# Edge attention on a graph: ScalarE's round in another order, one exp in place of two, and a third PSUM bank for small results

## The chip, the core and the metric

One core of a Trainium2 chip runs the whole program. The metric is the device time of one execution in microseconds. A profiled execution adds a trace: every instruction of the engines TensorE (PE, its weight loads PEld), VectorE (DVE), ScalarE (ACT), GpSimd (POOL) and SyncE (SP), and every DMA.

## The reference

6250 nodes with 128 features, 206250 edges sorted by their destination, 8 heads of 16 columns.

```python
Qh, Kh, Vh = (h @ WQ), (h @ WK), (h @ WV)        # each [N, 8, 16]
Eh = edge_attr @ WE                              # [E, 8, 16]
score = einsum('ehd,ehd,ehd->eh', Kh[src], Qh[dst], Eh) / sqrt(16)
score = exp(clip(score, -5, 5))
wV = segment_sum(Vh[src] * score[:, :, None], dst)
Z = segment_sum(score, dst)
x = layernorm(x + wV / (Z + 1e-6))
```

## The kernel before, in words

The edges lie in tiles of 128, one edge per partition, and four tiles are a batch: 406 batches, the last few of them smaller. First TensorE makes a table kv (K and V of each node, 256 columns) and stores it to HBM. Then one loop runs over the batches, and in each step every engine works at a different batch. In the steady part the code's order is each engine's order (`manual_schedule`).

- **Rows of the source nodes** (`gather`): GpSimd issues one indirect DMA per tile, which reads 128 rows of kv into the tile kvrows. 1426 of them are issued: a few tiles per batch are made in other ways. One is a *column tile*: VectorE and ScalarE copy x's columns one by one into xcol (`run`, `columns`), TensorE multiplies xcol by the weights into the PSUM tile colkv (`project_columns`), and ScalarE places the result in kvrows (`place_columns`). In a few batches SyncE loads the rows of one tile one by one. The first gather of a batch b from 18 on is held back until TensorE has done Q's rows of batch b - lag(b):

```python
return max(STEP, 12 - (b - LOCK) // 32)          # lag(b): STEP 3, LOCK 18
```

- **Q's rows** (`stage_0t`, `mark_t`, `stage_a`): TensorE makes marks_t, ScalarE turns it into onehotT by a Relu, and TensorE multiplies onehotT by a window of Q's table into qps. marks_t has one PSUM bank, so the next batch's marks_t waits for this onehotT. `build_q` makes the table, with qrows in PSUM and four VectorE instructions.
- **Scores** (`products`, `scores`): VectorE multiplies kvrows by qps, and that by eps (the edges' features times WE), sums by head and clips: sc, 32 columns per batch. qps and eps have one bank each.
- **Weights** (`weigh`): ScalarE takes exp of sc twice, once into exp_p, a single tile in PSUM, and once into the last 8 columns per tile of msg (128 + 8 columns, in SBUF, three buffers).
- **Messages** (`messages`): VectorE multiplies V's half of kvrows by exp_p, each of the 8 weights repeated over 16 columns, into the first 128 columns of msg.
- **Sums** (`stage_0`, `mark`, `stage_c`): TensorE makes marks, ScalarE the one-hot of the destinations, one for two batches, and TensorE multiplies it by msg into agg. ScalarE copies agg out (sum), `finish` shifts the sums into place (finps) for a block of 128 nodes, and VectorE's `layernorm` is spread over the steps by `fill`.

In step b VectorE runs the products of b - 1, the scores of b - 2 and the messages of b - 3, with pieces of columns between them. ScalarE's part of the step begins with the exps of b - 2. The PSUM pool psT (tag oT) has two banks, which marks, colkv, finps and qrows take in turn. The messages of b - 3 read exp_p, and the exps of b - 2 write it again in the same step.

Of the kernel before, what the change touches and what calls it, by code (L numbers as in the profile page):

```python
# [8 lines left out]
F32 = mybir.dt.float32  # L9
# [3 lines left out]
AF = mybir.ActivationFunctionType  # L13
ALU = mybir.AluOpType
AX = mybir.AxisListType

P = 128
N, E, D, H, DH = 6250, 206250, 128, 8, 16
NT = (E + P - 1) // P
EPAD = NT * P  # L20
B = 4
# [125 lines left out]
def edge_attention(ctx: ExitStack, tc: tile.TileContext, x, xT, srcT, srcA, srcV, srcR, dstT, dstB, dst0, bnd, loB, onB, onQ, eaT,  # L147
                   wq, wkv, we, out, kv, qtab, qs, relD, relO):
    nc = tc.nc
# [27 lines left out]
    nbat = len(batches)  # L177
# [9 lines left out]
    with ExitStack() as fast:  # L187
# [104 lines left out]
        sp = fast.enter_context(tc.tile_pool(name="sums", bufs=7))  # L292
        psE = fast.enter_context(tc.tile_pool(name="psE", bufs=1, space=bass.MemoryType.PSUM))
        psQ = fast.enter_context(tc.tile_pool(name="psQ", bufs=1, space=bass.MemoryType.PSUM))
        psT = fast.enter_context(tc.tile_pool(name="psT", bufs=2, space=bass.MemoryType.PSUM))
        psA = fast.enter_context(tc.tile_pool(name="psA", bufs=2, space=bass.MemoryType.PSUM))
        psX = fast.enter_context(tc.tile_pool(name="psX", bufs=1, space=bass.MemoryType.PSUM))
        psM = fast.enter_context(tc.tile_pool(name="psM", bufs=1, space=bass.MemoryType.PSUM))
        rows5 = [cp.tile([MR, P], BF16, name=f"rows5{i}") for i in range(3)]
        for tl in rows5:  # L300
            nc.vector.memset(tl, 1.0)
        exp_p = psX.tile([P, B, H], F32, name="exp_p")

        def pair_bank(i, name, shape):

# [75 lines left out]
        def load_rel(c):  # L381

            if c < NJ and c not in rels:
                rels[c] = rows_q[c % 3]
                nc.sync.dma_start(rels[c][:3], relD[c])
# [4 lines left out]
        def load_chunk(c):  # L390
            if c in chunks or c * CH >= NT:
                return
            n = min(CH, NT - c * CH) * P
            tl = ep.tile([P, CH * P], F32, name="ea")
            nc.sync.dma_start(tl[:, :n], eaT[:, c * CH * P:c * CH * P + n])
            chunks[c] = tl
# [35 lines left out]
        def due(b, v, part):  # L432

            n = int((b + part - 1 - COL0 + COLL) * COLP[1] * share[v] / COLP[0] + 1e-6) // (1 + v) * (1 + v)
            return min(n, len(col_batches) * share[v])

        def copy(v):

            c, (k, i) = copied[v] % COLN, divmod(copied[v], share[v])
            if c == 0:  # L440
                addresses(v)
                at_hand[v] = ahead[v].pop(0)
            copied[v] += 1 + v
            if k not in col_tiles:
                col_tiles[k] = wp.tile([P, P], F32, name="xcol", bufs=6)
            to, at = col_tiles[k], at_hand[v]
            if v:
                i += share[0]
                nc.vector.tensor_tensor(to.bitcast(I32)[:, i:i + 2], column(at[c], 8, I32),  # L449
                                        column(at[c + 1], 8, I32), op=ALU.bitwise_or)  # L450
            else:
                nc.scalar.copy(to[:, i:i + 1], column(at[c], 4, F32))  # L452

        def columns(b, part=1.0):

            while copied[0] < due(b, 0, part):
                copy(0)
# [45 lines left out]
        def place_columns():  # L503

            while projected:
                g, pk = projected.pop()
                nc.scalar.copy(g[:, B - 1, :], pk)  # L507
# [39 lines left out]
        def load_rows(c):  # L547

            if c < NJ and c not in rows_in:
                rows_in.add(c)  # L550
                nc.sync.dma_start(rows5[c % 3][:3 * WT], relO[c].rearrange("r (t e) -> (r t) e", t=WT))
# [48 lines left out]
        def mark_t(b):  # L600

            if b not in marks_t:
                return
            m, n = marks_t.pop(b)
            ohTs[b] = wp.tile([QROWS, B * P], BF16, name="onehotT", bufs=4)
            nc.scalar.activation(ohTs[b][:, :n * P], m[:, :n * P], AF.Relu)  # L606
# [35 lines left out]
        def weigh(b):  # L642

            n, g, sc = st8[b]
            nc.scalar.activation(exp_p[:, :n], sc[:, :n], AF.Exp, scale=0.25)  # L645
            m = wp.tile([P, B, MW], F32, name="msg")
            nc.scalar.activation(m[:, :n, D:], sc[:, :n], AF.Exp, scale=0.25)  # L647
            st8[b] = [n, g, m]
# [27 lines left out]
        def messages(b):  # L676
            n, g, m = st8[b]
            nc.vector.tensor_tensor(  # L678
                m[:, :n, :D].rearrange("p b (h d) -> p b h d", h=H),
                g[:, :n, D:].rearrange("p b (h d) -> p b h d", h=H),  # L680
                exp_p[:, :n, :, None].to_broadcast([P, n, H, DH]), op=ALU.mult)

        def stage_c(b):
            (n, g, m), oh = st8.pop(b), ohs.pop(b)
# [70 lines left out]
        for b in range(nbat + 4):  # L755
            on = b < nbat
            if b >= XB and not manual:
                manual.append(fast.enter_context(tc.manual_schedule()))
            held += [(b + SLAG, store) for store in stores]
            stores.clear()  # L760
            if held and (held[0][0] <= b or b >= nbat):
                held.pop(0)[1]()
            if b < nbat:
                load_chunk(batches[b][0] // CH + EB - 3)
                if batches[b][0] % WT == 0:
                    load_rows(batches[b][0] // WT + 1)
                    load_rel(batches[b][0] // WT + 2)
                load_q(batches[b][0] // WT + QLOOK)
                g = gathered.pop(b)
                if b == min(XB, nbat - 1):  # L770
                    late_loads()
                if b in (12, 13):
                    next(window, None)
                if b == 14:
                    for _ in window:
                        pass
                    window = from_window(1) if NJ > P else iter(())
                    next(window, None)
                if b >= 20 and b % 4 == 0:
                    next(window, None)  # L780
                if b == 0:
                    for u in range(min(2, nbat)):
                        stage_0t(u)
                        mark_t(u)
                stage_a(b, g)
                if b + GLEAD < nbat and b + GLEAD not in gathered:
                    gathered[b + GLEAD] = gather(b + GLEAD)
            norms.extend(late)
            late[:] = pending
            pending.clear()  # L790
            if b >= nbat:
                norms.extend(late)
                late.clear()
            made = products(b - 1) if 0 <= b - 1 < nbat else iter(())
            summed = scores(b - 2) if 0 <= b - 2 < nbat else iter(())
            if on and b >= XB:
                load_single(b, 0.5)
            next(made, None)
            for _ in run(b, 0.5) if on else ():
                fill(False)  # L800
            fill(False)
            next(made, None)
            next(summed, None)
            for _ in run(b, 1.0) if on else ():
                fill()
            fill()
            fill()
            next(summed, None)
            if 0 <= b - 3 < nbat:
                messages(b - 3)  # L810
            if 0 <= b - 2 < nbat:
                weigh(b - 2)
            while qwork and b > XB and qwork[0][1] < 3:
                build_q(0, False)
            place_columns()
            if 0 <= b - 1 < nbat:
                stage_0(b - 1)
            if b + 2 < nbat:
                stage_0t(b + 2)
            if b < nbat:  # L820
                columns(b)
            mark(b - 1)
            if b + 2 < nbat:
                mark_t(b + 2)
            for _ in range(len(ready) if b >= nbat - 2 else 1):
                if ready:
                    finish(ready.pop(0))
            if b == min(60, nbat):
                count_inside()
            if 0 <= b - 3 < nbat:  # L830
                stage_c(b - 3)
            if b < nbat:
                load_single(b, 1.0)
                project_columns(b + GLEAD)
                place_rows(b + GLEAD)
                build_q(q_built(min(NJ - 1, batches[b][0] // WT + QLOOK + 2)), True)
                if not qwork and len(built) < q_built(
                        min(NJ - 1, batches[min(nbat - 1, b + 3)][0] // WT + QLOOK + 2)):
                    qwork.append([q_rows(len(built)), 1])
                    next(qwork[0][0])  # L840
            if b == min(80, nbat + 1):
                inside = nc.values_load(cnt_i[0:1, 0:1], min_val=0, max_val=2 * EPAD,
                                        skip_runtime_bounds_check_because="two counts of EPAD edges")
# [190 lines left out]
```

## Time and profile before

| | us |
|---|---|
| median of three runs | 1878.13 |
| lowest and highest | 1872.55, 1889.53 |
| the profiled execution | 1871.11 |
| its span | 1869.3 |

| engine | busy us | share of the span |
|---|---|---|
| VectorE | 1648.0 | 88% |
| TensorE | 1499.8 | 80% |
| ScalarE | 1495.3 | 80% |
| GpSimd | 1359.8 | 73% |

A row of a group reads: line, engine, operation, out<-in by the program's names, shapes, count; then the busy time of all and the mean of one in ns; then the engine's idle time just before them, and what ended most of it. "issue" is idle time for which the profile shows no releaser. A row of a timeline begins with start and duration in us. A row of stretches has the stretch, its length, the busy time, the count in brackets, TensorE's granted clock, the DMA share and GB/s. A row of waits has the waiting instruction, the releaser, the total, the count and the longest.

### The profile page before, as it was taken

To read this page: it belongs to the slowest core of one execution; us is meant where nothing else is said; L and a number is where in the kernel's file an instruction comes from. 1 tells how busy PE (TensorE), PEld (TensorE's weight loads), DVE (VectorE), ACT (ScalarE), POOL (GpSimd) and SP (SyncE) were. 2 spreads that over 40 slices of the span, in tenths; PEclk is the share of its full clock that TensorE was granted. 3 is DMA by queue.
4 is the path that set the end of the run, shared out by engine and by line. 5 is a ranking of instruction groups with operands and counts; after the bars stand their busy time and mean duration, and the time that the engine had idled before them with its cause. 6 is when DMAs were issued, how large, how long until landed. Compare 5 with 4: busy or idle time off the path is not lost.

```text
span 1869.3 us, 54198 instructions
## 1 busy us (share of the span) xinstructions
PE 1499.8 (80%) x10000; PEld 1206.9 (65%) x10000; DVE 1648.0 (88%) x8774; ACT 1495.3 (80%) x11631; POOL 1359.8 (73%) x1433
## 2 busy tenths in 40 slices
PE   6898878878787888888887878877888878777886
PEld 4676657666666666666676666756766656666765
DVE  6468998898889988999989999899899899999986
ACT  3446888788898888898888888888888988988962
POOL 7767767777777776777766777777777777777774
PEclk9888898899899998999989999899989999999897
DMA  8655556556555655655555556556555556566652
GB/s 292 214 163 161 163 173 188 165 179 183 170 178 177 183 172 162 184 180 174 181 173 163 177 174 183 176 167 177 173 174 180 179 175 185 177 178 183 198 153 67
DMA packets 169255, 329.59 MB, mean 176 GB/s; under 512 B 67440, under 2 KB 95156, under 8 KB 168904
## 3 DMA queue, kind: packets, MB, share of 16 engines
q0 software_dynamic: 67664, 183.79, 33.0%
q1 hardware_dynamic: 100115, 141.48, 24.9%
q14 instruction: 272, 2.22, 0.4%
q8 instruction: 80, 1.31, 0.3%
q10 hardware_dynamic: 1124, 0.79, 0.1%
HBM read 309.03 MB, written 16.88 MB: 174 GB/s over the span
## 4 chain that ended last, share of the span: by engine, by line
DVE 34%; ACT 17%; PE 13%; DMA 8%; issue 7%; DVEq 6%; POOL 4%; SPq 2%; ACTq 2%; POOLq 0%
ACT xcol L452 12%; DVE xcol L449 10%; DMA kvrows<-kv,src 7%; DVEq L420 6%; DVE kq L629 5%; DVE sc L636 5%; DVE msg L678 5%; DVE kq L627 5%; POOL kvrows L518 4%; PE agg L700 4%; PE eps L620 3%; ACT onehot L584 2%; PE finps L659 2%; ACT onehotT L606 2%; ACTq L420 1%
## 5 line engine op out<-in xcount | busy, mean ns | idle before, releaser
L518 POOL DMA_INDIRECT kvrows<-kv,src x1378 | 1309.8, 950 | 471.6 <-issue 308.0
L452 ACT COPY xcol<-xz 128x1 f32 x9802 | 991.4, 189 | 76.9 <-issue 66.9
L700 PEld LDWEIGHTS agg<-msg,onehot 128*128 128x128 f32 x3224 | 436.0, 203 | 318.3 <-DVE msg L678 119.1
L449 DVE TENSOR_TENSOR xcol<-xz 128x2 int32 x5915 | 508.9, 152 | 60.5 <-issue 58.3
L620 PE MATMUL eps<-we_sb,ea 128*128 128x128 f32 x3224 | 489.4, 298 | 71.8 <-DVE kq L629 69.8
L700 PE MATMUL agg<-msg,onehot 128*128 128x136 f32 x3224 | 518.5, 307 | 32.3 <-DVE msg L678 30.6
L620 PEld LDWEIGHTS eps<-we_sb,ea 128*128 128x128 f32 x3224 | 424.2, 205 | 100.4 <-DVE kq L629 94.5
L627 DVE TENSOR_TENSOR kq<-kvrows,qps 128x512 f32<-128x512 f32 x406 | 273.8, 674 | 63.5 <-PE qps L615 38.8
L597 PE MATMUL marks_t<-rows_q,steps_q 5*126 5x512 bf16 x406 | 161.8, 399 | 169.5 <-ACT onehotT L606 155.5
L629 DVE TENSOR_TENSOR kq<-kq,eps 128x512 f32<-128x512 f32 x406 | 271.1, 668 | 8.6 <-PE eps L620 6.5
L678 DVE TENSOR_TENSOR msg<-kvrows,exp_p 128x512 f32<-128x512 f32 x406 | 272.7, 672 | 6.2 <-ACT exp_p L645 6.2
L636 DVE TENSOR_REDUCE sc<-kq 128x32 f32<-128x512 f32 x406 | 271.9, 670 | 0.3
L606 ACT ACTIVATE onehotT<-marks_t 126x512 bf16<-126x512 f32 x406 | 235.9, 581 | 19.2 <-PE marks_t L597 18.9
L645 ACT ACTIVATE exp_p<-sc 128x32 f32<-128x32 f32 x406 | 80.9, 199 | 193.9 <-DVE msg L678 191.1
L615 PE MATMUL qps<-qw,onehotT 126*128 126x128 bf16 x1612 | 168.8, 229 | 10.9 <-DVE kq L627 10.9
L615 PEld LDWEIGHTS <-onehotT 126*128 126x128 bf16 x1612 | 134.5, 103 | 47.8 <-issue 21.7
L500 PE MATMUL colkv<-wkv_sb,xcol 128*128 128x256 f32 x338 | 116.2, 429 | 17.2 <-ACT onehot L584 17.2
L584 ACT ACTIVATE onehot<-marks 128x512 f32<-128x512 f32 (+2 forms) x206 | 119.0, 577 | 5.5 <-PE marks L563 5.4
L659 PEld LDWEIGHTS finps<-sum,shift 128*128 128x128 f32 x640 | 81.4, 198 | 40.3 <-ACT kvrows L507 20.9
L659 PE MATMUL finps<-sum,shift 128*128 128x136 f32 x640 | 91.4, 296 | 9.5 <-ACT kvrows L507 9.5
L647 ACT ACTIVATE msg<-sc 128x32 f32<-128x32 f32 x406 | 88.5, 218 | 0.0
L639 DVE TENSOR_SCALAR sc<-sc 128x32 f32<-128x32 f32 x406 | 80.9, 199 | 0.9
(88 smaller groups left out, 799.3 us busy)
## 6 DMA issues: line engine op xcount, KB each, us to landing
ea<-eaT SPq DMA_DIRECT2D x201, 512.0 KB
rowkv<-kv SPq DMA_DIRECT2D x2176, 1.0 KB
kvrows<-kv,src POOLq DMA_INDIRECT x1378
qw<-qs SPq DMA_DIRECT2D x202, 31.5 KB
kv<-ea SPq DMA_DIRECT2D x12, 512.0 KB
qs<-qst SPq DMA_DIRECT2D x48, 96.0 KB
rows_q<-relD SPq DMA_DIRECT2D x202, 6.0 KB
rows<-relO SPq DMA_DIRECT2D x202, 6.0 KB
```

The costliest lines, as they stand in the source:

```text
L449: nc.vector.tensor_tensor(to.bitcast(I32)[:, i:i + 2], column(at[c], 8, I32), column(at[c + 1], 8, I32), op=ALU.bitwise_or)
L452: nc.scalar.copy(to[:, i:i + 1], column(at[c], 4, F32))
L518: ins = nc.gpsimd.indirect_dma_start(out=g[:k, i, :f], out_offset=None, in_=rows, in_offset=bass.IndirectOffsetOnAxis(ap=src_col(t)[:k], a ...
L606: nc.scalar.activation(ohTs[b][:, :n * P], m[:, :n * P], AF.Relu)
L615: expanded[b] = nc.tensor.matmul(pq[:, i, :], ohT[:, i * P:i * P + P], loaded[t0 // WT], start=True, stop=True)
L620: nc.tensor.matmul(pe[:, i, :], ea[:, i * P:i * P + P], we_sb, start=True, stop=True)
L627: nc.vector.tensor_tensor(t0[:, :n], g[:, :n, :D], pq[:, :n], op=ALU.mult)
L629: nc.vector.tensor_tensor(t0[:, :n], t0[:, :n], pe[:, :n], op=ALU.mult)
L636: nc.vector.tensor_reduce(sc[:, :n], t0[:, :n].rearrange("p b (h d) -> p b h d", h=H), axis=AX.X, op=ALU.add)
L659: nc.tensor.matmul(ps, shift[:, P - s:2 * P - s], sums[k // 2][:, k % 2], start=first and i == 0, stop=stop and i == len(parts) - 1)
L678: nc.vector.tensor_tensor(m[:, :n, :D].rearrange("p b (h d) -> p b h d", h=H), g[:, :n, D:].rearrange("p b (h d) -> p b h d", h=H), exp_p[ ...
L700: nc.tensor.matmul(aggs[u][:, 0 if final else k % 2], oh[:, i, :], m[:, i, :], start=not final and t % (2 * G) == 0, stop=tail)
```

## The change

Three things: the exp into exp_p and its tile are gone, and the messages read the weights from msg's own last columns; psT has three banks, the third being the one that exp_p had; and the place of three calls in the step is another, so that ScalarE runs the one-hots first, then the exps, the placing of column tiles and the columns.

```diff
-        psT = fast.enter_context(tc.tile_pool(name="psT", bufs=2, space=bass.MemoryType.PSUM))
+        psT = fast.enter_context(tc.tile_pool(name="psT", bufs=3, space=bass.MemoryType.PSUM))
...
-        psX = fast.enter_context(tc.tile_pool(name="psX", bufs=1, space=bass.MemoryType.PSUM))
...
-        exp_p = psX.tile([P, B, H], F32, name="exp_p")
...
             n, g, sc = st8[b]
-            nc.scalar.activation(exp_p[:, :n], sc[:, :n], AF.Exp, scale=0.25)
             m = wp.tile([P, B, MW], F32, name="msg")
             nc.scalar.activation(m[:, :n, D:], sc[:, :n], AF.Exp, scale=0.25)
...
                 g[:, :n, D:].rearrange("p b (h d) -> p b h d", h=H),
-                exp_p[:, :n, :, None].to_broadcast([P, n, H, DH]), op=ALU.mult)
+                m[:, :n, D:, None].to_broadcast([P, n, H, DH]), op=ALU.mult)
...
-            if 0 <= b - 2 < nbat:
-                weigh(b - 2)
             while qwork and b > XB and qwork[0][1] < 3:
                 build_q(0, False)
-            place_columns()
             if 0 <= b - 1 < nbat:
                 stage_0(b - 1)
             if b + 2 < nbat:
                 stage_0t(b + 2)
-            if b < nbat:
-                columns(b)
             mark(b - 1)
             if b + 2 < nbat:
                 mark_t(b + 2)
+            if 0 <= b - 2 < nbat:
+                weigh(b - 2)
+            place_columns()
+            if b < nbat:
+                columns(b)
```

ScalarE, about a step and a half late in the program, before (L645 and L647 are the exps, L452 the columns, L420 loads of the columns' addresses, L507 the placing of a column tile, L584 and L606 the one-hots):

```order
L645 ACTIVATE exp_p<-sc 128x32
L647 ACTIVATE msg<-sc 128x4x8
L507 COPY kvrows<-colkv 128x256
L452 COPY xcol<-xz 128x1 x2
L420 TENSOR_LOAD col_at_82
L452 COPY xcol<-xz 128x1 x16
L420 TENSOR_LOAD col_at_82
L452 COPY xcol<-xz 128x1 x9
L584 ACTIVATE onehot_78<-marks 128x2x4x64
L606 ACTIVATE onehotT<-marks_t 126x512
```

The same step now (lines are two or three lower from here on: L582 and L604 are the one-hots, L644 the exp, L505 the placing, L450 the columns):

```order
L582 ACTIVATE onehot_78<-marks 128x2x4x64
L604 ACTIVATE onehotT<-marks_t 126x512
L644 ACTIVATE msg<-sc 128x4x8
L505 COPY kvrows<-colkv 128x256
L450 COPY xcol<-xz 128x1 x2
L418 TENSOR_LOAD col_at_82
L450 COPY xcol<-xz 128x1 x16
L418 TENSOR_LOAD col_at_82
L450 COPY xcol<-xz 128x1 x9
```

The two one-hots moved from the end of the step to its start, one exp of the two is left, and the copies behind them are the same.

VectorE, one step late in the program, before (L639 is the clip, L678 the messages, L627 and L629 the two products, L449 pieces of columns, L636 the sum by head):

```order
L639 TENSOR_SCALAR sc<-sc 128x32
L678 TENSOR_TENSOR msg<-kvrows,exp_p 128x4x128
L627 TENSOR_TENSOR kq<-kvrows,qps 128x512
L420 TENSOR_LOAD col_at_83
L449 TENSOR_TENSOR xcol<-xz 128x2 x8
L629 TENSOR_TENSOR kq<-kq,eps 128x512
L636 TENSOR_REDUCE sc<-kq 128x32
```

And now:

```order
L637 TENSOR_SCALAR sc<-sc 128x32
L675 TENSOR_TENSOR msg<-kvrows,msg 128x4x128
L625 TENSOR_TENSOR kq<-kvrows,qps 128x512
L418 TENSOR_LOAD col_at_83
L447 TENSOR_TENSOR xcol<-xz 128x2 x8
L627 TENSOR_TENSOR kq<-kq,eps 128x512
L634 TENSOR_REDUCE sc<-kq 128x32
```

Nothing moved on VectorE; the messages' second operand is msg in place of exp_p. The rows of TensorE and GpSimd are the same in the steady part of both programs.

## The prediction

> **What bounds the kernel now.** I read the page first, for who is busy and with what.
>
> ```profile
> span 1869.3 us, 54198 instructions
> ...
> PE 1499.8 (80%) x10000; PEld 1206.9 (65%) x10000; DVE 1648.0 (88%) x8774; ACT 1495.3 (80%) x11631; POOL 1359.8 (73%) x1433
> ...
> DVE 34%; ACT 17%; PE 13%; DMA 8%; issue 7%; DVEq 6%; POOL 4%; SPq 2%; ACTq 2%; POOLq 0%
> ...
> L518 POOL DMA_INDIRECT kvrows<-kv,src x1378 | 1309.8, 950 | 471.6 <-issue 308.0
> ...
> L452 ACT COPY xcol<-xz 128x1 f32 x9802 | 991.4, 189 | 76.9 <-issue 66.9
> ...
> L678 DVE TENSOR_TENSOR msg<-kvrows,exp_p 128x512 f32<-128x512 f32 x406 | 272.7, 672 | 6.2 <-ACT exp_p L645 6.2
> ...
> L645 ACT ACTIVATE exp_p<-sc 128x32 f32<-128x32 f32 x406 | 80.9, 199 | 193.9 <-DVE msg L678 191.1
> ```
>
> By busy time VectorE leads with 88%, and its share of the chain, the line that begins with DVE, is the largest. GpSimd looks idle a quarter of the time. But the row of the gathers (L518) has 471.6 us of idle time that mostly nobody released ("issue"). So I read GpSimd next: the line's own view (durations as min/median/max), and from its timeline the first gather and a stretch near the end.
>
> ```profile
> L518 POOL DMA_INDIRECT kvrows<-kv,src x1378: 900/946/1912, 67.4 to 1847.5; - x197
> ...
> 3.62 1.11 POOL L518 DMA_INDIRECT kvrows<-x,src  x1 [2.06 <-DMA src<-srcT]
> ...
> 1739.86 0.95 POOL L518 DMA_INDIRECT kvrows<-kv,src  x1 [0.30 <-PE eps L620]
> ...
> 1847.52 0.90 POOL L518 DMA_INDIRECT kvrows<-kv,src  x1 [0.30 <-PE marks_t L597]
> ```
>
> From 1739.86 to 1847.52 us stand 87 gathers, 86 intervals, so one per 1.25 us: 0.946 of work, the median, and 0.304 that passes even where nobody is waited for. GpSimd is **saturated** there, whatever its busy share says. There are 1378 gathers from kv and 48 from x, 1426 in all, and 1426 x 1.25 = 1782.5 us. With 3.6 us before the first and 20.9 us behind the last (1847.52 + 0.90 to 1869.3) this makes 1807.0 us: the floor of this program while it issues 1426 gathers. The other 62.3 us are gathers that waited or took long. Where they waited, the groups of that engine in two stretches and in an early part of the first say:
>
> ```profile
> L518 POOL DMA_INDIRECT kvrows<-kv,src x922 | 875.9, 950 | 325.5 <-issue 208.9 <-PE qps L615 28.1 <-DVE qst L348 13.0
> ...
> L518 POOL DMA_INDIRECT kvrows<-kv,src x412 | 390.7, 948 | 128.3 <-issue 88.7 <-DVE sc L639 5.4 <-DVE xcol L449 3.7
> ...
> L518 POOL DMA_INDIRECT kvrows<-kv,src x189 | 181.3, 959 | 69.3 <-issue 47.6 <-PE marks_t L597 8.1 <-DVE kq L629 3.0
> ```
>
> The first row is the time from 130 to 1330 us. Less 0.304 us for each gather, 45.2 us of waiting are left. The second, 1330 to 1848 us, has 3.0 us left. The third, 130 to 380 us, has 11.8 of the first row's 45.2. The program holds each batch's first gather until TensorE has reached Q's rows of a batch some way back; that distance falls from 12 batches to 3. So up to 1330 us the other engines set the pace and GpSimd waits for them; behind that, GpSimd sets it. How fast the others go is counted by VectorE's first product (L627), one per batch; the x is the count:
>
> ```profile
> 1000.00:1300.00 300.00, 46.10 (x68) 0.95 0.58 175
> 1500.00:1800.00 300.00, 47.09 (x70) 0.97 0.61 183
> ```
>
> 68 batches in 300 us are 4.41 us each. GpSimd needs 1426 / 406 x 1.25 = 4.39 us per batch. The race is nearly even, so both sides of the change must be priced.
>
> **The change part by part.** *What it takes from the other engines.* The waits that it can end stand in the view of waits:
>
> ```profile
> ACT exp_p L645 <- DVE msg L678: 191.1, 143, 5.0
> PE marks_t L597 <- ACT onehotT L606: 155.5, 162, 2.3
> DVE kq L627 <- PE qps L615: 38.8, 30, 9.4
> DVE qst L348 <- PE qrows L344: 38.1, 29, 2.5
> PE qrows L344 <- ACT onehot L584: 21.0, 17, 2.3
> PE colkv L500 <- ACT onehot L584: 17.2, 17, 2.2
> PE finps L659 <- ACT kvrows L507: 9.5, 15, 1.0
> ```
>
> Dropping the first of the two exps takes 406 x 199 ns = 80.9 us from ScalarE, and with the single exp_p tile goes the wait for the messages, 191.1 us. Neither is on GpSimd's path, so by themselves they are worth nothing. Moving the one-hots ahead of the exps and the columns' copies takes away what TensorE waits for: onehotT no longer stands behind some 24 copies (9802 / 406), so most of the 155.5 us go. The third bank serves the last three rows, 21.0 + 17.2 + 9.5 = 47.7 us at most. These TensorE waits also count only by what they let VectorE do sooner: its waits for TensorE are 38.8 + 38.1 us, and 9.4 of them are one start-up wait that stays. That leaves 67.5 us, over 406 batches 0.17 us each. If all go, the pace is 4.41 - 0.17 = 4.24 us; if none, 4.41. I take most of it, since late onehotT and the two-bank rows stand directly ahead of these matmuls.
>
> The move has a wait of its own: ScalarE's round now starts at the one-hots, which need marks_t, a TensorE matmul behind the batch's edge products (eps). Behind them queue the exp, the placing of a column tile and the columns' copies. The exp is wanted by the messages one step (some 4 us) later and the columns several batches later, so I cost it at nothing. If the cover failed, VectorE would wait at the messages, where it now waits 6.2 us in all. VectorE's, TensorE's and GpSimd's orders are unchanged in the steady part, and no DMA moves, so no queue is passed.
>
> *What it costs: the messages read two SBUF tiles.* Their second operand was exp_p in PSUM and is now msg's own last 8 columns in SBUF. The instruction's length I bound from rows: 672 ns now (L678, 512 elements with one PSUM operand); the two-SBUF rows below, 0.41 us for 256 elements and 1.23 for 1024, put 512 at 0.68. At most 10 ns by 406, or 4 us of VectorE, which waits anyway. The larger cost is what such an instruction does to a gather:
>
> ```profile
> 122.26 1.23 DVE L233 TENSOR_TENSOR ea<-ea,relo 128x1024 f32<-128x1024 f32 x1
> ...
> 122.48 1.82 POOL L518 DMA_INDIRECT kvrows<-kv,src  x1 [4.73 <-DVE ea L232]
> ...
> 631.19 0.41 DVE L939 TENSOR_TENSOR h<-h,xb 128x256 f32<-128x256 f32 x1
> ...
> 631.23 1.19 POOL L518 DMA_INDIRECT kvrows<-kv,src  x1 [0.30 <-DVE h L936]
> ...
> 562.56 0.41 DVE L939 TENSOR_TENSOR h<-h,xb 128x256 f32<-128x256 f32 x1
> ...
> 562.45 0.95 POOL L518 DMA_INDIRECT kvrows<-kv,src  x1 [0.30 <-DVE h L936]
> ...
> 402.64 0.41 DVE L936 TENSOR_TENSOR h<-fin,rz 128x256 f32<-128x256 f32 x1
> ...
> 402.86 1.00 POOL L518 DMA_INDIRECT kvrows<-kv,src  x1 [0.30 <-issue]
> ```
>
> L233 and L939 read two SBUF tiles. The gather at 631.23 took 1.19 in place of 0.95, 0.24 more; L939 ended at 631.60, so the gather stood still from 631.36, 0.13 us behind its start, to that end. At 122.48 the same: 0.87 longer, L233's end at 123.49, so again 0.13 behind the start. At 562.45 the product began 0.11 us after the gather, and nothing happened. So a gather needs something at 0.13 us that a two-SBUF product holds, once that product has begun by about 0.03 us ahead of the gather (the latest that stretched one, at 631.19, by 0.04). A message of 0.67 us then catches a gather whose start lies in a window of 0.67 - 0.13 - 0.03 = 0.51 us out of each 1.25, that is 41% of them, and delays it half of 0.51 on the mean: 0.41 x 0.255 = 0.105 us per message, 42.6 us for 406. Bounds: nothing, if the tile's strided operand does not hold it, and 0.51 x 406 = 207 us, if every message caught a gather at the worst place. I take 42.6, the value for no fixed phase, since the messages keep none now:
>
> ```profile
> 1001.38 0.68 DVE L678 TENSOR_TENSOR msg<-kvrows,exp_p 128x512 f32<-128x512 f32 x1
> ...
> 1005.63 0.67 DVE L678 TENSOR_TENSOR msg<-kvrows,exp_p 128x512 f32<-128x512 f32 x1
> ...
> 1009.31 0.67 DVE L678 TENSOR_TENSOR msg<-kvrows,exp_p 128x512 f32<-128x512 f32 x1
> ```
>
> They follow each other by 4.25 and by 3.68 us, which leaves 0.50 and 1.18 over whole intervals of 1.25.
>
> The Trainium skill, GPSIMD Engine Reference, Key points, states this against the change: GpSimd shares its SBUF interfaces with VectorE and contends with instructions that have two SBUF inputs. The rows above agree and add the price, which the page lacks; had the whole message counted each time, 406 x 0.67 = 272 us would come on top.
>
> *The sum.* GpSimd now needs 4.39 + 0.105 = 4.50 us per batch. While the allowed distance shrinks by 9 batches over 288, the others let it go at 297 / 288 = 1.031 times their own pace: 4.55 us now, above 4.39, hence the waits; 4.37 at 4.24, below 4.50, hence none. Of the 45.2 us I keep 6 for the early part, and the 4.73 of 122.48 and the 3.0 stay. So 1869.3 - 39.2 + 42.6 = **1872.7 us** of span. What lies around the span was 1.8 us (profiled run 1871.11): 1874.5, say 1875. Against that run it is 0.2% more; the median of the three runs, 1878.13, lies 7 us above the profiled one, and they scatter by 17. The gain is real, and it is paid back at GpSimd.
>
> **The rivals.**
> 1. *The messages do not hold up the gathers*, because the operand is a repeated 8-column piece, or they fall beside them. For it: the third pair of rows. Against it: L936, whose second operand (rz) is 8 columns repeated in the same way, also stretches one, at 402.86 (1.00, and not 0.95; L936 ended 0.19 behind its start). Then 1869.3 - 39.2 = 1830 of span, 1832; with half the delay 1853.
> 2. *The others do not get faster*: ScalarE's new wait for marks_t replaces the one on the messages, and the change does not do what it says. The pace stays 4.41, GpSimd's waits swallow the delay up to 1330 us (4.55 against 4.50), and only the 118 batches behind it pay: 118 x 0.105 = 12.4, so 1881.7 of span, 1884.
> 3. *The two rhythms lock*, and the time ends above before. Once the lead is used up, VectorE starts each batch when its last gather lands, so the message sits at one place of the 1.25 us. If that is inside the window, each message costs 0.255 and not 0.105 us. Over the last half of the batches that is 203 x 0.15 = 30 us more: 1905. It decides from a mean of 0.145 us per message, where the time passes 1890. Against it: transfers land after unequal times, as two pieces of the chain show, which smears the phase.
>
> ```profile
> 790.29 4.75 DMA kvrows<-kv,src
> ...
> 1217.89 2.61 DMA kvrows<-kv,src
> ```
>
>
> **How the numbers follow.** A change of 1% is about what a measurement of this kernel tells from none. Forecast (1855 to 1890): 0.50. Rival 1, 0.20; rival 2, 0.15; rival 3, 0.15. Faster by over 1%, below 1852, comes from rival 1 and a little of the forecast's edge: 0.24. Slower by over 1%, above 1890, from rival 3, a part of rival 2 and the other edge: 0.22. Within: 0.54. The range reaches from just above rival 1's full gain, 1838, to rival 3's price, 1905; outside I leave the full form of rival 1 and the worst of rival 3.
>
> **What would show it.** GpSimd: the gathers' mean rises from 950 ns by 42.6 / 1426 x 1000 = 30 to about 980, with the long ones under messages, and their idle beyond 0.304 us each falls from 53 (471.6 - 1378 x 0.304) to about 14 us. ScalarE: 406 fewer instructions and no wait for messages. TensorE: the wait for onehotT under 30 us. VectorE: messages of 672 to 682 ns, and new waits for gathered rows late in the run. A gathers' mean near 950 would make rival 1 right, waits that stay at 40 us rival 2. Wrong altogether would be a loss on TensorE or ScalarE that I have as covered.

## The result, and the profile after

The changed kernel takes 1891.23 us, the kernel before 1877.84 us (medians of 12 runs each). The ratio is **1.0081, 95% interval 1.0058 to 1.0105**: slower by 0.8%. The prediction had 1875 us, and 1855 to 1890 for its forecast: the time lies 16 us above the one and 1 us above the other. It is still within 1% of the kernel before, because that kernel's median lies 7 us above the one profiled run, 1871.11 us, from which the prediction counted. The profiled execution took 1890.43 us, 1888.6 of them its span, 19.3 more than before.

The page of the changed kernel has these lines (L516 is the gather, L595 marks_t, L604 onehotT, L675 the messages, L644 the exp, L625 the first product; the columns are those of the page of before):

```profile
span 1888.6 us, 54050 instructions
...
PE 1573.2 (83%) x10000; PEld 1264.1 (67%) x10000; DVE 1654.7 (88%) x8774; ACT 1444.9 (77%) x11225; POOL 1424.7 (75%) x1433
...
L516 POOL DMA_INDIRECT kvrows<-kv,src x1378 | 1373.9, 997 | 428.3 <-issue 313.0
...
L675 DVE TENSOR_TENSOR msg<-kvrows,msg 128x512 f32<-128x512 f32 x406 | 274.9, 677 | 6.8 <-ACT msg L644 6.4
...
L595 PE MATMUL marks_t<-rows_q,steps_q 5*126 5x512 bf16 x406 | 173.7, 428 | 3.6 <-ACT onehotT L604 2.1
```

The one line that answers the question is that of the gathers. Their mean went from 950 to 997 ns, and their busy time by 1373.9 - 1309.8 = 64.1 us; their idle time went from 471.6 to 428.3, 43.3 us less waiting. The last gather ends at 1869.94 in place of 1848.42, so the tail is 18.7 and not 20.9 us. The 48 gathers from x took 0.7 us more (49.8 and 49.1). 64.1 + 0.7 - 43.3 - 2.2 = 19.3 us, the whole difference of the spans.

The two stretches of GpSimd's groups that the prediction used, for the changed kernel (the second one now to 1870 us):

```profile
L516 POOL DMA_INDIRECT kvrows<-kv,src x919 | 916.9, 998 | 284.0 <-issue 210.5 <-PE marks_t L595 9.2 <-DVE xcol L447 8.5
...
L516 POOL DMA_INDIRECT kvrows<-kv,src x415 | 413.4, 996 | 126.5 <-issue 91.1 <-DVE sc L634 4.9 <-DVE sc L637 4.6
```

Up to 1330 us the waits beyond 0.304 us per gather are 284.0 - 919 x 0.304 = 4.6 us, where they were 45.2. GpSimd now sets the pace from one end to the other. The view of waits agrees from the other engines' side:

```profile
ACT onehot L582 <- PE marks L561: 159.8, 101, 6.6
...
ACT onehotT L604 <- PE marks_t L595: 152.5, 106, 4.9
...
DVE kq L625 <- PE qps L613: 32.0, 17, 7.2
DVE kq L625 <- DMA kvrows<-kv,src: 31.7, 31, 4.2
...
DVE qst L346 <- PE qrows L342: 10.4, 8, 2.9
```

TensorE's 155.5 us for onehotT are gone (2.1 are left). ScalarE waits 312 us for TensorE's marks, in place of 191 for the messages, and no other engine waits more than 7.3 us in all for one of its lines. VectorE waits 31.7 us for gathered rows, where it waited 13.4.

Why the gathers are long, and longer than forecast, stands in the timelines. First three consecutive messages, then the gathers about them:

```profile
563.26 0.68 DVE L675 TENSOR_TENSOR msg<-kvrows,msg 128x512 f32<-128x512 f32 x1
...
567.50 0.69 DVE L675 TENSOR_TENSOR msg<-kvrows,msg 128x512 f32<-128x512 f32 x1
...
571.79 0.69 DVE L675 TENSOR_TENSOR msg<-kvrows,msg 128x512 f32<-128x512 f32 x1
```

```profile
563.34 1.43 POOL L516 DMA_INDIRECT kvrows<-kv,src  x1 [0.30 <-DVE y L943]
565.07 0.95 POOL L516 DMA_INDIRECT kvrows<-kv,src  x1 [0.30 <-issue]
566.32 0.95 POOL L516 DMA_INDIRECT kvrows<-kv,src  x1 [0.30 <-issue]
567.57 1.44 POOL L516 DMA_INDIRECT kvrows<-kv,src  x1 [0.30 <-DVE w L947]
569.32 0.95 POOL L516 DMA_INDIRECT kvrows<-kv,src  x1 [0.30 <-issue]
570.57 0.96 POOL L516 DMA_INDIRECT kvrows<-kv,src  x1 [0.30 <-issue]
571.83 1.47 POOL L516 DMA_INDIRECT kvrows<-kv,src  x1 [0.30 <-issue]
```

Each message begins less than 0.1 us ahead of a gather and holds it to the message's end: 563.34 + 0.13 to 563.94 is 0.47, and the gather took 1.43, 0.48 more than 0.95. Then two gathers pass, and the next is caught at the same place. What the prediction worked out for one gather holds to some 10 ns; the places are not evenly spread. In the kernel before, where the messages read exp_p in PSUM, 187 gathers had this moment, 0.13 us behind their start, under a message, and none of them took more than 0.02 us longer.

### The profile page after: what moved, and what is told of

The parts are those of the page before. It is cut to its first block, busy times and chain, and to the rows that moved or that the text cites. A ratio compares the mean times of both kernels' runs of the same rounds, so it can differ in the third digit from the quotient of the medians.

```text
span 1888.6 us, 54050 instructions
## 1 busy us (share of the span) xinstructions
PE 1573.2 (83%) x10000; PEld 1264.1 (67%) x10000; DVE 1654.7 (88%) x8774; ACT 1444.9 (77%) x11225; POOL 1424.7 (75%) x1433
## 4 chain that ended last, share of the span: by engine, by line
DVE 46%; PE 14%; DMA 10%; DVEq 7%; issue 5%; POOL 4%; ACT 1%; SPq 1%; ACTq 0%; POOLq 0%
DVE xcol L447 13%; DMA kvrows<-kv,src 9%; DVE kq L627 8%; DVE kq L625 7%; DVEq L418 7%; DVE sc L634 7%; DVE msg L675 5%; PE agg L697 4%; PE eps L618 4%; POOL kvrows L516 4%; PE finps L656 3%; DVE sc L637 2%; ACT xcol L450 1%; PE colkv L498 1%; PE marks_t L595 1%
## 5 line engine op out<-in xcount | busy, mean ns | idle before, releaser
L516 POOL DMA_INDIRECT kvrows<-kv,src x1378 | 1373.9, 997 | 428.3 <-issue 313.0
L450 ACT COPY xcol<-xz 128x1 f32 x9802 | 987.7, 191 | 44.3 <-issue 33.8
L618 PE MATMUL eps<-we_sb,ea 128*128 128x128 f32 x3224 | 510.1, 306 | 156.6 <-DVE kq L627 153.4
L697 PE MATMUL agg<-msg,onehot 128*128 128x136 f32 x3224 | 533.4, 313 | 95.7 <-DVE msg L675 95.2
L697 PEld LDWEIGHTS agg<-msg,onehot 128*128 128x128 f32 x3224 | 450.5, 209 | 224.7 <-DVE msg L675 190.0
L618 PEld LDWEIGHTS eps<-we_sb,ea 128*128 128x128 f32 x3224 | 438.4, 211 | 200.6 <-DVE kq L627 191.0
L604 ACT ACTIVATE onehotT<-marks_t 126x512 bf16<-126x512 f32 x406 | 238.7, 588 | 157.8 <-PE marks_t L595 152.5
L625 DVE TENSOR_TENSOR kq<-kvrows,qps 128x512 f32<-128x512 f32 x406 | 274.4, 676 | 88.3 <-PE qps L613 32.0
L627 DVE TENSOR_TENSOR kq<-kq,eps 128x512 f32<-128x512 f32 x406 | 271.5, 669 | 10.7 <-PE eps L618 9.0
L675 DVE TENSOR_TENSOR msg<-kvrows,msg 128x512 f32<-128x512 f32 x406 | 274.9, 677 | 6.8 <-ACT msg L644 6.4
L582 ACT ACTIVATE onehot<-marks 128x512 f32<-128x512 f32 (+2 forms) x206 | 120.4, 584 | 160.3 <-PE marks L561 159.8
L595 PE MATMUL marks_t<-rows_q,steps_q 5*126 5x512 bf16 x406 | 173.7, 428 | 3.6 <-ACT onehotT L604 2.1
L656 PEld LDWEIGHTS finps<-sum,shift 128*128 128x128 f32 x640 | 99.0, 234 | 23.3 <-issue 21.9
L656 PE MATMUL finps<-sum,shift 128*128 128x136 f32 x640 | 110.8, 336 | 0.5 <-ACT sum L708 0.5
L644 ACT ACTIVATE msg<-sc 128x32 f32<-128x32 f32 x406 | 91.1, 224 | 1.5 <-DVE sc L637 1.2
L561 PE MATMUL marks<-steps,rows 26*128 26x512 bf16 (+2 forms) x206 | 84.6, 411 | 0.0
```

The costliest lines, as they stand in the source:

```text
L516: ins = nc.gpsimd.indirect_dma_start(out=g[:k, i, :f], out_offset=None, in_=rows, in_offset=bass.IndirectOffsetOnAxis(ap=src_col(t)[:k], a ...
L618: nc.tensor.matmul(pe[:, i, :], ea[:, i * P:i * P + P], we_sb, start=True, stop=True)
L625: nc.vector.tensor_tensor(t0[:, :n], g[:, :n, :D], pq[:, :n], op=ALU.mult)
L627: nc.vector.tensor_tensor(t0[:, :n], t0[:, :n], pe[:, :n], op=ALU.mult)
L656: nc.tensor.matmul(ps, shift[:, P - s:2 * P - s], sums[k // 2][:, k % 2], start=first and i == 0, stop=stop and i == len(parts) - 1)
L675: nc.vector.tensor_tensor(m[:, :n, :D].rearrange("p b (h d) -> p b h d", h=H), g[:, :n, D:].rearrange("p b (h d) -> p b h d", h=H), m[:, : ...
```

## The experiments

The first four ran on one chip, with the kernel before at 1877.37 us. Theory A is the prediction's: GpSimd's gathers set the end, and the messages' two SBUF operands hold them up. Its rivals are B, the new order of ScalarE's round makes the loss, and C, the third bank carries the gain.

### The new order alone

```diff
(of before)
-            if 0 <= b - 2 < nbat:
-                weigh(b - 2)
...
-            place_columns()
...
-            if b < nbat:
-                columns(b)
             mark(b - 1)
             if b + 2 < nbat:
                 mark_t(b + 2)
+            if 0 <= b - 2 < nbat:
+                weigh(b - 2)
+            place_columns()
+            if b < nbat:
+                columns(b)
```

> The new order of ScalarE's round alone: both exps, exp_p in PSUM, two psT banks, messages read exp_p. Theory A (GpSimd's gathers set the end, and messages with two SBUF inputs hold them up): no gather is lengthened by a message, mean near 950 ns; the new order lets the others go faster, GpSimd's waits beyond 0.304 us fall from 53 to under 25 us; span 1835 to 1850, about 2% below before. Theory B (the new order itself makes the loss, ScalarE's wait for marks_t): span near 1885, gathers still 950 ns, GpSimd waiting 60 us and more. Theory C (the third bank brought what was gained): waits stay near 50 us, span near 1869.

Measured: 1843.48 us, ratio 0.9841 (0.9789 to 0.9893), span 1837.9. Its gathers:

```profile
L518 POOL DMA_INDIRECT kvrows<-kv,src x1378 | 1309.5, 950 | 442.5 <-issue 309.5 <-PE qps L615 17.1 <-DVE sc L639 15.3
```

The mean is the 950 ns of before, and the waits are 442.5 - 1378 x 0.304 = 23.6 us, where they were 52.7. B falls: the order alone gains 1.6%. C falls as the main cause, for there is no third bank here. This kernel beats both.

### The exps' part alone

```diff
(of before)
-        psX = fast.enter_context(tc.tile_pool(name="psX", bufs=1, space=bass.MemoryType.PSUM))
...
-        exp_p = psX.tile([P, B, H], F32, name="exp_p")
...
-            nc.scalar.activation(exp_p[:, :n], sc[:, :n], AF.Exp, scale=0.25)
...
-                exp_p[:, :n, :, None].to_broadcast([P, n, H, DH]), op=ALU.mult)
+                m[:, :n, D:, None].to_broadcast([P, n, H, DH]), op=ALU.mult)
```

> The exps' part alone: one exp, messages read msg's own columns, old order of ScalarE's round, two psT banks, exp_p gone. Theory A: messages lengthen gathers by 45 to 65 us in sum, and the other engines go little faster than before since onehotT still stands behind the columns; GpSimd's waits fall by less than that; span 1885 to 1900. Theory B (order makes the loss): span at or below before's 1869, as ScalarE only loses work and a wait.

Measured: 1889.56 us, ratio 1.0063 (1.0033 to 1.0092), span 1885.3, and the loss is there without the new order:

```profile
L516 POOL DMA_INDIRECT kvrows<-kv,src x1378 | 1373.8, 997 | 422.5 <-issue 297.2 <-DMA kvrows<-kv,src 13.7 <-DVE sc L637 13.7
```

997 ns again: 64.0 us of lengthening, without the new order. GpSimd has hardly a wait left (422.5 against 418.9 of bare gaps), though TensorE still waited 93.5 us for onehotT. That the others became faster, with one exp and one wait fewer on ScalarE, is not needed for this: with 0.158 us more per batch the gathers need 4.55 us, as much as the prediction gave for the pace that the others, unchanged, leave GpSimd up to 1330 us. The prediction's sum for engines that are no faster (rival 2), with the measured price, is 1869.3 + 118 x 0.158 = 1887.9 us, near this span and near the changed kernel's 1888.6. So once the messages hold the gathers, no gain of the new order can be seen (1.0063 and 1.0081, with intervals that overlap).

### The messages in two halves

```diff
(of the changed kernel)
-            nc.vector.tensor_tensor(m[:, :n, :D] ..., g[:, :n, D:] ..., m[:, :n, D:, None] ...)
+            for i in range(0, n, 2):
+                k = min(2, n - i)
+                nc.vector.tensor_tensor(m[:, i:i + k, :D] ..., g[:, i:i + k, D:] ..., m[:, i:i + k, D:, None] ...)
```

> The change whole, but each batch's messages as two instructions of 256 elements. Theory A: a 0.41 us instruction holds a gather for at most 0.41 - 0.16 = 0.25 us, so the lengthening falls from 65 to 20 to 35 us, while VectorE gets some 0.07 us per batch more; span 1850 to 1865. Rival (what counts is the whole time that VectorE spends with two SBUF inputs): lengthening stays near 65 us, span 1888 or more.

Measured: 1867.83 us, ratio 0.9940 (0.9916 to 0.9963), span 1866.0. A useful half-way house: faster than the changed kernel with the same work in more instructions.

```profile
L516 POOL DMA_INDIRECT kvrows<-kv,src x1378 | 1348.7, 979 | 430.5 <-issue 302.1 <-DVE sc L634 16.5 <-DVE msg L677 15.2
```

The gathers are busy for 38.9 us more than before, a little more than the 20 to 35 expected, and the span lies 1 us above its range. One reason stands in the timeline: a gather caught by the first half is not always let through before the second (the first row holds both halves). In the trace 38 gathers were held to the end of the second half so, and 36 to that of the first.

```profile
616.18 0.75 DVE L677 TENSOR_TENSOR msg<-kvrows,msg 128x256 f32<-128x256 f32 x2
```

```profile
616.23 1.52 POOL L516 DMA_INDIRECT kvrows<-kv,src  x1 [0.30 <-DVE xcol L447]
```

1.52 is 0.57 more than 0.95, and 616.23 + 0.13 + 0.57 is 616.93, the end of the second half. The rival, that all time with two SBUF inputs counts, falls with the 25 us that went.

### The change without its third bank

```diff
(of the changed kernel)
-        psT = fast.enter_context(tc.tile_pool(name="psT", bufs=3, space=bass.MemoryType.PSUM))
+        psT = fast.enter_context(tc.tile_pool(name="psT", bufs=2, space=bass.MemoryType.PSUM))
```

> The change without its third psT bank. Theory A: GpSimd sets the end with or without it, span 1885 to 1892, lengthening near 65 us, GpSimd's waits under 20 us. Theory C (the bank carries the gain): GpSimd's waits return to 30 us or more and the span goes to 1905 or above.

Measured: 1891.52 us, ratio 1.0081 (1.0045 to 1.0117), span 1889.7, gathers of 998 ns. It can't be told from the change whole: theory A was right, and C, which wanted 30 us of waits, falls (428.9 - 418.9 = 10.0). TensorE did wait for the bank again (finps for the one-hot: 13.4 us), off the path. What the bank is worth where GpSimd does not set the end was not tried, as exp_p needs a bank of its own.

### A lock of two rhythms?

The forecast had 42.6 us of lengthening, and 64.1 were measured. So I counted the changed kernel's message rows by their distance from the message before, with the lengthening of the gather that each holds:

| distance, us | messages | gathers held | lengthening, us | per message |
|---|---|---|---|---|
| 3.6 to 3.8 | 146 | 9 | 4.6 | 0.03 |
| 4.15 to 4.35 | 75 | 64 | 28.8 | 0.38 |
| all others | 184 | 94 | 32.8 | 0.18 |

The sum, 66.2 us, is 2 us more than the 64.1, since two of these gathers were held by other products as well.

A plain step of VectorE is 3.68 us, a step with a block's layernorm in it 4.24. Against three gathers, 3.75 us, the first is 0.07 short and slips out of the window; the second is 0.49 over, which is just the delay that it causes. Theory L: a held gather starts the gathers' rhythm anew from the message's end, so the next message finds it at a place that VectorE's own step sets. The changed kernel's rows show this directly: behind a message that held a gather, the next one at 4.15 to 4.35 us held one again in 51 of 53 cases, for 0.49 us in the median, and the next one at 3.6 to 3.8 us in none of 55. Behind a message that held none it was 13 of 22 and 9 of 91. To tell this from an accident (theory U), another instruction is put behind the messages, which does nothing but change the step:

```diff
(of the changed kernel, and of the new order alone)
+        pad = cp.tile([P, 1], F32, name="pad")
...
+            nc.vector.tensor_reduce(pad, iota_f[:, :32], axis=AX.X, op=ALU.add)
```

The first try ran on a chip where every kernel took a third longer, the kernel before 2552.69 us.

> The change whole, and behind each batch's messages one more small VectorE instruction, a sum of 32 elements to one, some 0.1 us of extra step and no use otherwise. In the changed kernel 74 messages end 4.15 to 4.35 us behind the one before and lengthen gathers by 28.8 us, 0.39 each; 146 end 3.6 to 3.8 us behind and lengthen them by 4.6. Theory L (lock: a held gather sets the gathers' rhythm by the message's end, and 4.24 us of step is three gathers of 1.25 and 0.49, so the next one is held again by 0.49): with steps of 4.34 the message begins after the gather's moment and the runs of long gathers break; the lengthening falls from 66 to some 40 us and the span to 1860 to 1875, though VectorE has 40 us more to do. Theory U (no lock, the excess over 42.6 us is a wider window or an accident): lengthening stays at 60 to 70 us and the span at 1888 or above.

> The new order alone with the same small instruction behind the messages, which read exp_p in PSUM here: the control for the added instruction. No gather is lengthened either way, so theory L and theory U both expect it to bring nothing: span 1838 to 1860, at or above that of the new order alone, with GpSimd waiting more than its 24 us.

There the changed kernel with the instruction had a ratio of 0.9831 (0.9772 to 0.9890), the new order with it 0.9995 (0.9955 to 1.0035). In the first one GpSimd waited 1068.8 - 418.9 = 650 us of 2515, and the two kernels without the instruction have no run on this chip, so neither theory was tested:

```profile
L517 POOL DMA_INDIRECT kvrows<-kv,src x1378 | 1349.5, 979 | 1068.8 <-issue 334.5 <-PE qps L614 310.6 <-PE eps L619 109.3
```

So both ran again, with the kernel before at 1876.87 us.

> The change whole, with one more small VectorE instruction of some 0.1 us behind each batch's messages, once more, on a chip where the kernel before runs near 1877 us. There the gathers are one per 1.25 us from end to end, which theory L needs; on the chip of the first try they were not (GpSimd waited 660 us of 2515), and there the lengthening was 40 us. Theory L (lock): lengthening falls from 66 to some 40 us, the runs of 0.49 us are gone, span 1860 to 1875. Theory U (no lock): lengthening 60 to 70 us, span 1888 or above.

> The new order alone with the small VectorE instruction behind the messages, once more, as the control: both theories expect nothing from it, span 1838 to 1860, no gather lengthened by a message.

Measured: the changed kernel with the instruction 1881.84 us, 1.0033 (1.0013 to 1.0052), span 1879.6; the new order with it 1868.87 us, 0.9970 (0.9951 to 0.9988), span 1864.8. **The same useless instruction made the changed kernel some 0.5% faster (1.0081 to 1.0033) and the control 1.3% slower (0.9841 to 0.9970).** The gathers of the first and of the control, then the first one's plain steps and the gathers at the ends of these messages:

```profile
L517 POOL DMA_INDIRECT kvrows<-kv,src x1378 | 1362.9, 989 | 430.5 <-issue 309.4 <-DVE sc L638 16.8 <-DMA kvrows<-kv,src 11.6
```

```profile
L519 POOL DMA_INDIRECT kvrows<-kv,src x1378 | 1311.8, 952 | 466.1 <-issue 315.6 <-PE qps L616 29.4 <-DVE sc L640 18.0
```

```profile
594.32 0.68 DVE L676 TENSOR_TENSOR msg<-kvrows,msg 128x512 f32<-128x512 f32 x1
...
598.08 0.68 DVE L676 TENSOR_TENSOR msg<-kvrows,msg 128x512 f32<-128x512 f32 x1
...
601.85 0.68 DVE L676 TENSOR_TENSOR msg<-kvrows,msg 128x512 f32<-128x512 f32 x1
```

```profile
594.86 0.96 POOL L517 DMA_INDIRECT kvrows<-kv,src  x1 [0.30 <-PE marks_t L596]
...
598.63 0.96 POOL L517 DMA_INDIRECT kvrows<-kv,src  x1 [0.30 <-DVE sc L638]
...
602.38 0.96 POOL L517 DMA_INDIRECT kvrows<-kv,src  x1 [0.30 <-DVE sc L638]
```

The plain step grew by 0.08 us to 3.76 and now runs beside three gathers, with next to no delay. The lengthening fell to 1362.9 - 1309.8 = 53.1 us, the part of the distances from 4.15 to 4.35 from 28.8 to 19.0. The messages are as long as before (679 ns), so the lengthening depends on VectorE's step. The size was missed: theory L expected 40 us and a span up to 1875, theory U 60 us or more and 1888, and the run lies between them. Theory L had counted on steps of 4.34 us; those with layernorm and no idle time came out at 4.25 to 4.29 in the median, and of the 67 messages 4.15 to 4.35 us behind the one before 31 still delayed a gather by 0.44 us or more. What decides for the lock is the count of 51 of 53 and 0 of 55 above; this run agrees with it. The control came out 5 us above its range: its span is 26.9 us longer than without the instruction, near 406 x 0.08 = 32, and its GpSimd waits rose to 466.1 - 418.9 = 47 us. So the added work costs time where no gather is held, and the gain in the changed kernel isn't the instruction's own.

### Fewer gathers

```diff
(of the new order alone)
-COLP = (11,5)
+COLP = (2,1)
...
-COLV = 70
+COLV = 64
```

> The new order alone (exps and banks as before), and a column tile in every second batch in place of 5 of 11: 186 in place of 169, so 17 gathers fewer, with 64 of a tile's 128 columns on VectorE and 64 on ScalarE in place of 70 and 58. If GpSimd sets the end there too, 17 x 1.25 = 21 us less than the new order alone: span near 1817. If the other engines do by then (ScalarE gets some 0.5 us more per batch, VectorE the same), span at or above 1838.

> The new order alone with 186 column tiles in place of 169, 17 gathers fewer, once more, on a chip where the kernel before runs near 1877 us. If GpSimd sets the end: span near 1817. If ScalarE, with 0.5 us more per batch, or another engine does: 1838 or above.

The ratio was 1.0253 (1.0195 to 1.0312) on the slow chip and 1.0425 (1.0358 to 1.0492), 1954.13 us, on the other. The floor of GpSimd went down and another took its place:

```profile
L452 ACT COPY xcol<-xz 128x1 f32 x11904 | 1177.0, 189 | 50.9 <-issue 41.7
```

```profile
by line: ACT xcol L452 32.3%; PE finps L659 5.3%; ACT onehotT L606 5.2%; DMA kvrows<-kv,src 4.5%; issue 3.8%; DVE xcol L449 3.7%; PE agg L700 3.5%; ACTq L420 3.1%; ACT onehot L584 3.1%; PE eps L620 3.0%; DVE kq L629 2.4%; DVEq L420 2.4%; DV
```

ScalarE's column copies, 1177.0 us in place of 991.4, hold a third of the chain. So GpSimd stays the bound only while ScalarE has room for more copies, and gathers traded for copies in this way do not pay.

## Why the prediction was right and wrong

- **GpSimd's saturated queue as the bound: right.** Gathers that nothing holds still come one per 1.25 us, and the span's 19.3 us are their lengthening less their waits and the shorter tail.
- **The gain of the new order: right where it stands alone; in the sum the number came out for a reason that isn't shown.** TensorE's wait for onehotT was to be under 30 us and is 2.1. With the new order alone VectorE did 209 batches between 400 and 1300 us in place of 203, 4.31 us each in place of 4.43; the sum had 4.24. In the changed kernel it did 204. GpSimd's waits were to fall from 53 to about 14 us and fell to 428.3 - 1378 x 0.304 = 9.4, but without the new order they fell to 3.6, as the longer gathers alone use them up. So the 39.2 us of the sum fit the changed kernel partly by luck.
- **ScalarE's new wait costs nothing: right.** It waits 312 us for TensorE's marks, and the messages wait 6.4 us for it, where they waited 6.2.
- **The third bank counts only through VectorE: not tested.** Without it the time is the same, but GpSimd sets the end in both kernels.
- **The messages' length, 672 to 682 ns: right,** 677.
- **The price of the second SBUF operand: right in kind, too small.** This is the step that failed: "I take 42.6, the value for no fixed phase, since the messages keep none now". 64.1 us came, 0.158 per message and not 0.105. The share of messages that hold a gather was as forecast (167 of 406, 41%), but each delays it by 0.40 us, not 0.255. The spacing in the profile of before was no evidence, because nothing tied the gathers to the messages there; once a message can hold a gather, it sets the gathers' phase itself, and steps of 4.24 us meet it where it costs most. With 64.1 in the sum in place of 42.6, and 9.4 of waits left in place of 13.7, it comes to 1872.7 + 21.5 - 4.3 = 1889.9 of span, and to 1887.7 with the tail that is 2.2 shorter; 1888.6 were measured.
- **Rival 3, the lock, was the right correction with the wrong cause.** It expected the lock once the lead was used up, from the rows' landing. The long gathers stand already between 130 and 380 us, where GpSimd is some nine batches ahead (26 of the 55 messages there hold one); it is VectorE's own step that sets the place. Its price of 30 us over the forecast is near the 21.5 that came. A mean of 0.145 us per message was where it let the time pass 1890; 0.158 were measured, and the time is 1891.23.
- **Rival 1** is ruled out by the long gathers. **Rival 2**, that the others do not get faster, is ruled out by the run of the new order alone (0.9841); the waits that went do not tell, since they went without the new order too.

## What to carry to other kernels

Add up an engine's instructions and the fixed gaps between them before calling it idle: 75% busy can be a full queue. Before an operand of a VectorE instruction moves from PSUM to SBUF, so that both inputs lie in SBUF, look whether GpSimd is issuing indirect DMAs beside it and look in the trace for gathers that such an instruction already stretches. Where one event can push a periodic one, don't price it by an even spread of phases: the push itself sets the next meeting, so take the step lengths that occur and see what they leave over whole periods.

## What the runs showed of the hardware

- A gather is held at one moment, 0.126 us behind its start, until the two-SBUF product over it ends; its time is then 0.946 us + (end of the product - start of the gather - 0.126), within 10 ns in 161 of the 167 cases of the changed kernel. Of eight products that began up to 0.07 us behind the gather's start two held it; those that began 0.13 us or more behind it did not. The Trainium skill (GPSIMD Engine Reference, Key points) names this contention; these runs agree and give its price.
- Two such products back to back can hold the same gather through both (1.52 us above; 38 gathers in that run).
- One chip ran the kernel before at 2552.69 us in place of 1877, at a granted clock of TensorE of 0.74 to 0.77 (the three kernels profiled there) in place of 0.89 to 0.93, with gathers and VectorE instructions as long as elsewhere (a gather 951 ns, a message 676, in the new order with the added instruction). What made it slow stays open.
